# Splitting a place in a list at 64 instead of 128: smaller one-hots, more values, results written in two halves

## The chip, the cores and the metric

The kernel runs on one core of a Trainium2 chip. A core has a matrix engine (TensorE, in the profile PE, with its weight loads shown apart as PEld), a vector engine (VectorE, DVE), a scalar engine (ScalarE, ACT), a general engine (GpSimd, POOL) and SyncE (SP), which issues most of the transfers. Each engine works through its own list of instructions in order and waits on semaphores for the others. The metric is the device time of one execution in microseconds (us), the median of several runs. The profile comes from one further execution.

## What is computed

Four graph-attention layers over 4096 nodes with 256 features and one adjacency matrix of 4096 x 4096, in which about one entry in 256 is set, more of them for nodes with low numbers. Each layer normalises, projects, forms a softmax over the neighbours of every node, and adds the result to x. The first layer stands for all:

```python
h = jnp.maximum(_layernorm(x, axis=-1), 0.0)
h = h @ W.T + b_W
e = (h @ a1)[:, None] + (h @ a2)[None, :] + b_a[0]
e = jnp.where(e > 0, e, 0.2 * e)
scores = jnp.where(adj > 0, e, NEG_INF)
x = x + jax.nn.softmax(scores, axis=1) @ h
```

The second layer ends with an elu, the third has four heads of 64 features, the fourth subtracts a second softmax of the negated scores and projects both.

## The kernel before

Targets are taken in tiles of 128 nodes (32 tiles), four tiles to a block. A target tile is worked on in one of two ways. Densely: all 32 source tiles are multiplied, with a mask. By lists: only those sources that some node of the target tile has as a neighbour. Target tiles with low numbers have many neighbours and stay dense (four blocks in the first layer); for the 28 tiles of blocks 1 to 7 the first layer also makes a list of sources, and the later layers use it. The first four source tiles are always taken whole; 28 source tiles (JT) remain to be listed.

For a list, the number of a used source has to stand at its place: source k-th in the list goes to partition k mod 128 and column k div 128 of a tile idx of 128 partitions and CAPS[T] columns (6 to 12). Each column of idx then drives one indirect transfer on POOL: 128 rows of the feature table (L1228) or of the mask table (L928) are gathered with it.

The function `list_sources` does this for one block of four target tiles. It is a Python generator: a pump advances it by one `yield` at a time in between the steps of the dense and listed multiplications, so that its instructions are issued among theirs. `seen` tells which sources are used; two small matmuls and some additions give every source its place in the list (posi); an unused source gets a place beyond any list. Then

- L857 and L858 split posi into its low part (and with 127) and its high part (shift by 7), and L860 and L862 turn both into f16;
- L865 makes val, a one-hot of the high part over MAXCAP = 12 columns, and L869 multiplies it with the source's own number (code);
- L875, in `one_hot`, makes first, a one-hot of the low part over 128 places, for half of the 28 source tiles at a time: two such instructions for each target tile, 56 in all, made one ahead of their use, in two buffers;
- L900 multiplies them: for each target tile, 28 matmuls of 128 sources each, first as the stationary and val as the moving operand, are added up in PSUM, so that the number of each source lands on its place. 28 tiles with 28 matmuls make 784;
- L910 writes the sum, with an offset and as integers, to idx.

The constants place (0 to 127, repeated) and lists (0 to 11, repeated), against which L865 and L875 compare, are written by POOL at the start in `list_constants` (L790, L794). POOL's order is the program's own; the instructions of the other engines are ordered by a scheduler when the kernel is compiled, so a change in one part can move others by some places.

Around the lists run the other parts of the first layer: L1303 loads pieces of the adjacency matrix, L1322 makes the mask of them (DVE), L1032 weighs mask and scores (DVE, tile s_p), L1068 multiplies weights and features (PE, tile s_acc), L716 and L748 transpose and project nodes for the next layer, L1119 to L1122 end a target tile. L580 is a group of 16 small matmuls for the third layer's weights, L640 of four for a bias, L829 and L830 the two matmuls that count list places. L1093 is the multiplication of the third layer.

Of the kernel before, what the change touches and what calls it, by code (L numbers as in the profile page):

```python
# [8 lines left out]
F32 = mybir.dt.float32  # L9
F16 = mybir.dt.float16  # L10
# [3 lines left out]
ALU = mybir.AluOpType  # L14
# [3 lines left out]
P = 128  # L18
# [5 lines left out]
IT = IB // P  # L24
# [432 lines left out]
JT = NT - DP  # L457
# [6 lines left out]
MAXCAP = max(CAPS[TS0:])  # L464
OFFS = [sum(CAPS[TS0:T]) for T in range(NT + 1)]
NLIST = OFFS[NT]
HALF = N // 2
# [12 lines left out]
def list_layers(ctx: ExitStack, tc: tile.TileContext, a: dict, out: bass.AP, flag):  # L480

    nc = tc.nc
# [8 lines left out]
    ps_mm = ctx.enter_context(tc.tile_pool(name="s_mm", bufs=2, space=PSUM))  # L491
# [15 lines left out]
        tri, onesb, pattern=[[1, P]], compare_op=ALU.is_gt, fill=0.0, base=0, channel_multiplier=-1  # L507
# [278 lines left out]

    def list_constants(pool):

        place = pool.tile([P, P, JT // 2], F16, name="place")
        nc.gpsimd.iota(  # L790
            place, pattern=[[1, P], [0, JT // 2]], base=0, channel_multiplier=0, allow_small_or_imprecise_dtypes=True
        )
        lists = pool.tile([P, MAXCAP, JT * IT], F16, name="lists")
        nc.gpsimd.iota(  # L794
            lists,
            pattern=[[1, MAXCAP], [0, JT * IT]],
            base=0,
            channel_multiplier=0,
            allow_small_or_imprecise_dtypes=True,
        )  # L800

        code = pool.tile([P, JT * IT], F16, name="code")
        n = (NT // 2 - DP) * IT
        for part, tiles, base in ((code[:, 0:n], NT // 2 - DP, DP * P - HALF), (code[:, n:], NT // 2, 1)):
            nc.gpsimd.iota(
                part,
                pattern=[[CH * P, tiles // CH], [1, CH], [0, IT]],
                base=base,
                channel_multiplier=CH,
                allow_small_or_imprecise_dtypes=True,  # L810
            )
        sums = []
        for k in range(2):
            t = pool.tile([P, NT // 2 + JT, IT], F32, name=f"sums_{k}")
            nc.gpsimd.memset(t[:, 0 : NT // 2, :], 0.0)
            sums.append(t)
        return place, lists, code, sums

    def list_sources(ib, seen, pool, consts):

        n = JT * IT
        place, lists, code, sums = consts
        half = JT // 2
        used = pool.tile([P, JT, IT], F16, name=f"used_{ib}", tag="used")
        nc.vector.tensor_scalar(used, seen, 0.0, None, op0=ALU.is_gt)
        yield 4.0
        uf = used.rearrange("p j t -> p (j t)")
        pre = ps_mm.tile([P, 2, JT, IT], F32, name=f"pre_{ib}", tag="mm")
        nc.tensor.matmul(pre[:, 0].rearrange("p j t -> p (j t)"), lhsT=tri, rhs=uf, start=True, stop=True)  # L829
        nc.tensor.matmul(  # L830
            pre[:, 1].rearrange("p j t -> p (j t)"), lhsT=onesb, rhs=uf, start=True, stop=True
        )
        yield

        z = NT // 2
        nc.vector.tensor_copy(sums[0][:, z:, :], pre[:, 1])
        pos = pool.tile([P, JT, IT], F32, name=f"pos_{ib}", tag="pos")
        nc.vector.tensor_sub(pos, pre[:, 0], sums[0][:, z:, :])
        k, a = 1, 0
        while k < JT:  # L840
            nc.vector.tensor_add(
                sums[1 - a][:, z:, :], sums[a][:, z:, :], sums[a][:, z - k : z + JT - k, :]
            )
            k, a = 2 * k, 1 - a
        yield
        t0 = ib * IT - TS0
        nc.vector.tensor_sub(
            over[:, t0 : t0 + IT], sums[a][:, z + JT - 1, :], places[:, t0 : t0 + IT]
        )
        nc.vector.tensor_add(pos, pos, sums[a][:, z:, :])  # L850

        nc.vector.tensor_scalar(pos, pos, 8192.0, None, op0=ALU.add)
        posi = pool.tile([P, JT, IT], I32, name=f"posi_{ib}", tag="posi")
        nc.vector.scalar_tensor_tensor(posi, used, -8192.0, pos, op0=ALU.mult, op1=ALU.add)
        yield
        low = pool.tile([P, 2, JT, IT], I32, name=f"low_{ib}", tag="low")
        nc.vector.tensor_scalar(low[:, 0], posi, P - 1, None, op0=ALU.bitwise_and)  # L857
        nc.vector.tensor_scalar(low[:, 1], posi, 7, None, op0=ALU.logical_shift_right)  # L858
        lof = pool.tile([P, IT, JT], F16, name=f"lof_{ib}", tag="lof")
        nc.vector.tensor_copy(lof, low[:, 0].rearrange("p j t -> p t j"))  # L860
        hib = pool.tile([P, n], F16, name=f"hib_{ib}", tag="hib")
        nc.vector.tensor_copy(hib, low[:, 1].rearrange("p j t -> p (j t)"))  # L862
        yield
        val = pool.tile([P, MAXCAP, n], F16, name=f"val_{ib}", tag="val")
        nc.vector.tensor_tensor(  # L865
            val, lists, hib.unsqueeze(1).to_broadcast([P, MAXCAP, n]), op=ALU.is_equal
        )
        yield
        nc.vector.tensor_tensor(val, val, code.unsqueeze(1).to_broadcast([P, MAXCAP, n]), op=ALU.mult)  # L869
        yield 4.0  # L870

        def one_hot(T, j):

            first = pool.tile([P, P, half], F16, name=f"first_{T}_{j}", tag="first", bufs=2)
            nc.vector.tensor_tensor(  # L875
                first,
                place,
                lof[:, T % IT, j : j + half].unsqueeze(1).to_broadcast([P, P, half]),
                op=ALU.is_equal,
            )  # L880
            return first


        ahead = [(ib * IT + t, j) for t in range(IT) for j in (0, half)]
        firsts = [one_hot(*ahead[0])]
        yield 4.0
        for t in range(IT):
            T = ib * IT + t
            cap = CAPS[T]
            ps = None  # L890
            for j in range(JT):
                if j % half == 0:
                    first = firsts.pop()
                    ahead.pop(0)
                    if ahead:
                        firsts.append(one_hot(*ahead[0]))
                    yield
                if ps is None:
                    ps = ps_mm.tile([P, MAXCAP], F32, name=f"idx_ps_{T}", tag="mm")
                nc.tensor.matmul(  # L900
                    ps[:, 0:cap],
                    lhsT=first[:, :, j % half],
                    rhs=val[:, 0:cap, j * IT + t],
                    start=(j == 0),
                    stop=(j == JT - 1),
                )
                if j % 7 == 6:
                    yield
            idx = keep.tile([P, cap], I32, name=f"idx_{T}", tag=f"idx_{T}")
            nc.vector.tensor_scalar(idx, ps[:, 0:cap], float(HALF), None, op0=ALU.add)  # L910
            index[T] = idx
            yield

# [331 lines left out]
    with ExitStack() as phase:  # L1245
# [33 lines left out]
        half = CH // 2  # L1279
# [31 lines left out]
        def mask_chunk(ib, c):  # L1311

            load()
            if ib == 0:
                behind(c)
            m = (
                mpre[:, :, ib * IB : (ib + 1) * IB]
                if c == 0
                else mpool.tile([P, CH, IB], U8, name=f"s_m_{ib}_{c}", tag="m")
            )  # L1320
            for h, raw in enumerate(loaded[ib, c]):
                nc.vector.tensor_scalar(m[:, h * half : (h + 1) * half, :], raw, 0.0, None, op0=ALU.is_gt)  # L1322
            if c > 0 or ib in MASKS_IN:
                nc.sync.dma_start(mask_rows(ib, c * CH), m)
            if ib > 0:
                if c == 0:
                    seen[ib] = lists_p.tile([P, JT, IT], F32, name=f"seen_{ib}", tag="seen", bufs=4)
                else:
                    nc.vector.tensor_reduce(
                        seen[ib][:, (c - 1) * CH : c * CH, :].rearrange("p j t -> p (j t)"),  # L1330
                        m.rearrange("p j i -> p (j i)")
                        .bitcast(I32)
                        .rearrange("p (t w) -> p t w", w=P // 4),
                        AX.X,
                        ALU.max,
                    )
                if c == NCH - 1:
                    push(lists_q, list_sources(ib, seen[ib], lists_p, consts))
            return m
# [31 lines left out]
        for b in range(1, 4):  # L1371
            load_x(b)
        consts = list_constants(lists_p)
        for _ in L0.making:
            pass
# [4 lines left out]
        for ib in range(DENSE[0]):  # L1380
            for step in block(ib).plan():
                plan.append(step)
                if ib * NT + step[1] >= LISTED0:
                    n = 1 + step[1] % 2
# [25 lines left out]
    for l in (1, 2, 3):  # L1410
# [37 lines left out]
        if l == 3:  # L1448
            one = Unit(L, 0, IT, NT, all_sources(L, 0, IT, [0], 1), big="growb", heads=[0])
            two = Unit(L, 0, IT, NT, all_sources(L, 0, IT, [1], 1), big="growb", heads=[1], like=one)  # L1450
            first = one.plan() + two.plan()
        else:
            per = L.H
            first = []
# [88 lines left out]
```

## Time and profile before

| | |
|---|---|
| Median of 3 runs | 1701.94 us (1697.17 to 1703.21) |
| The profiled execution itself | 1796.08 us |
| its span, first to last instruction | 1794.3 us |
| granted TensorE clock, mean over the span | 0.97 |
| List matmuls L900 | 784, first at 114.5, last at 499.1 us |
| Indirect transfers that read idx | 715 for features, 105 for masks |
| Adjacency loads L1303 | 128 of 512 KB |

The profiled execution is longer than the runs; durations of single instructions are taken from it and sums are made against it. A page of a profile gives, for each group of instructions, the line, the engine, the operation, the tiles written and read, shapes, count, the busy time in us and the mean of one in ns, and after the bar the time for which the engine stood idle just before, with what ended that. The chain of waits follows the work that ended last back to what released it. A share of busy time is an average over stages that have different limits, so it is the stage of the lists, from about 90 to 510 us, that has to be read. Matmul ends are modelled, so a burst of matmuls is best measured from its first start to the start of what follows.

### The profile page before, as it was taken

What the parts mean: (1) busy time and instruction counts of PE and PEld (TensorE: products, weight loads), DVE (VectorE), ACT (ScalarE), POOL (GpSimd) and SP (SyncE); (2) the same over time, 40 slices, a digit from 0 to 9 for tenths busy, and PEclk for the clock granted to TensorE, in tenths of its full rate; (3) what the DMA queues carried; (4) which work ended last, traced back from release to release, by engine and by line L of the source; (5) the groups of instructions that cost most, each with busy time, mean ns of one, the idle gap of its engine ahead of it and who ended that gap; (6) DMA issues with size and microseconds to landing.
All of it is one profiled execution on the core that took longest, in us unless ns stands there. A gap on an engine that the chain in (4) does not pass through costs nothing.

```text
span 1794.3 us, 29158 instructions
## 1 busy us (share of the span) xinstructions
PE 1660.2 (93%) x9268; PEld 1384.3 (77%) x9268; DVE 1319.1 (74%) x3908; ACT 631.0 (35%) x1915; POOL 960.5 (54%) x930
## 2 busy tenths in 40 slices
PE   6998899799889999888999999988889999999997
PEld 4886777678778778676577878788888888888876
DVE  6787899777744676556788888877785566777755
ACT  5630010020120232333467666788884011111101
POOL 8836666646535656553353444444561666655453
PEclk9999999999879999989999999999999999999999
DMA  7888778853244444543233332323342665666553
GB/s 258 301 299 281 242 244 251 264 143 110 60 135 138 134 117 134 147 132 106 82 94 86 90 90 81 98 82 83 99 116 75 197 208 175 183 180 178 160 165 107
DMA packets 152237, 274.70 MB, mean 153 GB/s; under 512 B 21423, under 2 KB 75340, under 8 KB 152076
## 3 DMA queue, kind: packets, MB, share of 16 engines
q0 software_dynamic: 45584, 130.39, 26.8%
q1 hardware_dynamic: 105656, 141.83, 24.2%
q8 instruction: 77, 1.26, 0.3%
q14 instruction: 84, 0.69, 0.1%
q10 hardware_dynamic: 836, 0.53, 0.1%
HBM read 231.76 MB, written 40.90 MB: 152 GB/s over the span
## 4 chain that ended last, share of the span: by engine, by line
PE 78%; DVE 8%; issue 4%; DMA 3%; POOL 3%; ACT 2%; another core or an unknown queue 2%; SPq 0%; POOLq 0%; DVEq 0%; ACTq 0%
PE s_acc L1068 44%; PE s_accm L1093 20%; PE s_pj L748 8%; DVE s_p L1032 3%; PE idx_ps L900 2%; PE s_tp L716 2%; PE s_sT L966 2%; DMA s_gg<-table,idx 1%; DMA s_raw<-in_adjT 1%; ACT s_p L1018 1%; DVE s_m L1322 1%; POOL s_z L702 1%; POOL s_gg L1228 1%; DVE s_p L1041 0%
## 5 line engine op out<-in xcount | busy, mean ns | idle before, releaser
L1228 POOL DMA_INDIRECT s_gg<-table,idx x715 | 757.9, 1060 | 733.5 <-PE s_acc L1068 228.6
L1032 DVE SCALAR_TENSOR_TENSOR s_p<-s_grow,s_gg,mlist 128x128 f32<-128x128 f32 x994 | 310.1, 346 | 143.0 <-PE s_acc L1068 85.9
L1068 PE MATMUL s_acc<-s_gg,s_p 128*128 128x257 f32 x1430 | 353.8, 390 | 9.9 <-DVE s_p L1032 7.8
L1068 PEld LDWEIGHTS s_acc<-s_gg,s_p 128*128 128x128 f32 x1430 | 270.5, 194 | 53.6 <-DVE s_p L1032 12.6
L1068 PE MATMUL s_acc<-g,s_p 128*128 128x257 f32 x1152 | 292.5, 397 | 14.2 <-DVE s_p L1032 5.3
L1068 PEld LDWEIGHTS s_acc<-g,s_p 128*128 128x128 f32 x1152 | 220.0, 198 | 49.7 <-issue 12.3
L1032 DVE SCALAR_TENSOR_TENSOR s_p<-s_grow,pre,mpre 128x128 f32<-128x128 f32 (+1 forms) x576 | 189.2, 369 | 49.4 <-PE s_acc L1068 30.5
L1093 PE MATMUL s_accm<-s_p,s_gg 128*65 128x128 f32 x1744 | 204.7, 273 | 1.7 <-issue 1.6
L1068 PE MATMUL s_acc<-s_gs,s_p 128*128 128x257 f32 x896 | 203.6, 380 | 0.0
L1032 DVE SCALAR_TENSOR_TENSOR s_p<-s_grow,s_gs,s_ms 128x512 f32<-128x512 f32 x224 | 161.9, 748 | 50.7 <-PE s_accm L1093 24.7
L748 PE MATMUL s_pj<-s_w,s_hT 128*128 128x259 f32 (+3 forms) x640 | 175.9, 417 | 24.9 <-ACT s_hT L718 9.5
L1093 PEld LDWEIGHTS s_accm<-s_p,s_gg 128*65 128x65 f32 x1744 | 193.2, 138 | 5.3 <-issue 2.8
L1018 ACT ACTIVATE s_p<-s_grow,s_minus,s_gg 128x128 f32<-128x128 f32 x436 | 186.7, 485 | 25.9 <-PE s_accm L1093 15.0
L1068 PE MATMUL s_acc<-pre,s_p 128*128 128x257 f32 x768 | 184.0, 384 | 5.5 <-ACT s_y L1179 3.5
L1068 PEld LDWEIGHTS s_acc<-s_gs,s_p 128*128 128x128 f32 x896 | 169.4, 190 | 24.7 <-issue 0.6
L972 ACT ACTIVATE s_grow<-s_sT 128x256 f32<-128x256 f32 (+2 forms) x136 | 46.8, 367 | 379.3 <-PE s_sT L966 260.9
L748 PEld LDWEIGHTS s_pj<-s_w,s_hT 128*128 128x128 f32 x640 | 126.3, 205 | 56.4 <-ACT s_hT L718 14.2
L1068 PEld LDWEIGHTS s_acc<-pre,s_p 128*128 128x128 f32 x768 | 144.5, 192 | 28.4 <-ACT s_y L1179 3.9
L928 POOL DMA_INDIRECT mlist<-mask_t,idx x105 | 122.1, 1162 | 65.1 <-issue 30.0
L1093 PE MATMUL s_accm<-s_p,pre 128*65 128x128 f32 (+1 forms) x928 | 122.2, 286 | 2.6 <-issue 2.5
L1093 PEld LDWEIGHTS s_accm<-s_p,pre 128*65 128x65 f32 x928 | 105.1, 139 | 21.0 <-issue 18.3
L1018 ACT ACTIVATE s_p<-s_grow,s_minus,pre 128x128 f32<-128x128 f32 x224 | 95.0, 485 | 23.2 <-issue 18.9
(126 smaller groups left out, 1743.5 us busy)
## 6 DMA issues: line engine op xcount, KB each, us to landing
s_raw<-in_adjT SPq DMA_DIRECT2D x128, 512.0 KB
s_gs<-table SPq DMA_DIRECT2D x28, 516.0 KB
s_gg<-table,idx POOLq DMA_INDIRECT x715
mask_t<-s_m SPq DMA_DIRECT2D x35, 256.0 KB
table<-s_g SPq DMA_DIRECT2D x28, 258.0 KB
s_ms<-mask_t SPq DMA_DIRECT2D x28, 256.0 KB
table<-s_m SPq DMA_DIRECT2D x21, 256.0 KB
table<-g SPq DMA_DIRECT2D x8, 516.0 KB
```

Source lines behind the costliest of these rows:

```text
L702: (nc.gpsimd if L.l == 0 else nc.vector).tensor_scalar(z, x[:, T, :], mv[:, k, 0:1], 0.0, op0=ALU.subtract, op1=ALU.max)
L716: nc.tensor.transpose(tp[:, c, :], zs[k][:, c * P : (c + 1) * P], ident)
L748: nc.tensor.matmul(ps, lhsT=hT[:, c, :], rhs=L.w[:, c, k * (D + 6) : k * (D + 6) + cols], start=(c == 0), stop=(c == 1),)
L900: nc.tensor.matmul(ps[:, 0:cap], lhsT=first[:, :, j % half], rhs=val[:, 0:cap, j * IT + t], start=(j == 0), stop=(j == JT - 1),)
L928: nc.gpsimd.indirect_dma_start(out=mlist[:, OFFS[T] + k, :], out_offset=None, in_=mask_t[T // IT], in_offset=bass.IndirectOffsetOnAxis(ap= ...
L966: nc.tensor.transpose(ps[:, h - h0, it, :], L.s[:, T0 + it, h : h + 1].to_broadcast([P, P]), ident)
L972: nc.scalar.activation(grow[:, h1:h2, :], ps[:, h1 - h0 : h2 - h0].rearrange("p h a b -> p h (a b)"), AF.Exp, scale=scale,)
L1018: nc.scalar.activation(w[:, h, :], u.grow[:, h, :], AF.Relu, scale=g[h][:, n - 1 : n], bias=minus)
L1032: nc.vector.scalar_tensor_tensor(p[:, k, :], u.grow[:, h, :], g[k][:, n - 1 : n], m, op0=ALU.min if L.l == 3 and h == 1 else ALU.max, op1= ...
L1068: nc.tensor.matmul(u.accs[it][h], lhsT=p[:, k, it * P : (it + 1) * P], rhs=g[k][:, 0:n], start=first, stop=last,)
L1093: nc.tensor.matmul(u.regions[h], lhsT=g[k][:, 0 : DH + 1], rhs=p[:, k, :],  start=first and (u.nt > 1 or h == 0), stop=last, skip_group_ch ...
L1228: nc.gpsimd.indirect_dma_start(out=wide, out_offset=None, in_=L.table, in_offset=bass.IndirectOffsetOnAxis(ap=index[T][:, k : k + 1], axis=0),
```

## The change

The place is split at 64: the low six bits choose one of 64 places, the rest one of 2 x MAXCAP = 24 columns. The one-hots first have half their size, the values val twice theirs; a matmul has 64 stationary columns and twice the moving columns (12 to 24), and its result has 64 partitions. Even columns of it belong to partitions 0 to 63 of idx, odd ones to 64 to 127, so the result is written with two instructions, one for each half. What idx holds is the same.

```diff
-        place = pool.tile([P, P, JT // 2], F16, name="place")
+        place = pool.tile([P, P // 2, JT // 2], F16, name="place")
...
-        lists = pool.tile([P, MAXCAP, JT * IT], F16, name="lists")
+        lists = pool.tile([P, 2 * MAXCAP, JT * IT], F16, name="lists")
...
-        nc.vector.tensor_scalar(low[:, 0], posi, P - 1, None, op0=ALU.bitwise_and)
-        nc.vector.tensor_scalar(low[:, 1], posi, 7, None, op0=ALU.logical_shift_right)
+        nc.vector.tensor_scalar(low[:, 0], posi, P // 2 - 1, None, op0=ALU.bitwise_and)
+        nc.vector.tensor_scalar(low[:, 1], posi, 6, None, op0=ALU.logical_shift_right)
...
-        val = pool.tile([P, MAXCAP, n], F16, name=f"val_{ib}", tag="val")
+        val = pool.tile([P, 2 * MAXCAP, n], F16, name=f"val_{ib}", tag="val")
         nc.vector.tensor_tensor(
-            val, lists, hib.unsqueeze(1).to_broadcast([P, MAXCAP, n]), op=ALU.is_equal
+            val, lists, hib.unsqueeze(1).to_broadcast([P, 2 * MAXCAP, n]), op=ALU.is_equal
         )
         yield
-        nc.vector.tensor_tensor(val, val, code.unsqueeze(1).to_broadcast([P, MAXCAP, n]), op=ALU.mult)
+        nc.vector.tensor_tensor(val, val, code.unsqueeze(1).to_broadcast([P, 2 * MAXCAP, n]), op=ALU.mult)
...
-            first = pool.tile([P, P, half], F16, name=f"first_{T}_{j}", tag="first", bufs=2)
+            first = pool.tile([P, P // 2, half], F16, name=f"first_{T}_{j}", tag="first", bufs=2)
...
-                    ps = ps_mm.tile([P, MAXCAP], F32, name=f"idx_ps_{T}", tag="mm")
+                    ps = ps_mm.tile([P // 2, 2 * MAXCAP], F32, name=f"idx_ps_{T}", tag="mm")
                 nc.tensor.matmul(
-                    ps[:, 0:cap],
+                    ps[:, 0 : 2 * cap],
                     lhsT=first[:, :, j % half],
-                    rhs=val[:, 0:cap, j * IT + t],
+                    rhs=val[:, 0 : 2 * cap, j * IT + t],
...
-            nc.vector.tensor_scalar(idx, ps[:, 0:cap], float(HALF), None, op0=ALU.add)
+            for k in range(2):
+                nc.vector.tensor_scalar(
+                    idx[k * P // 2 : (k + 1) * P // 2, :], ps[:, k : 2 * cap : 2], float(HALF), None, op0=ALU.add
+                )
```

The two iotas on POOL and the broadcasts of the comparisons follow these sizes.

More of the change, by code (lines that the diff above doesn't have):

```diff
@@ L787, in list_constants @@
     def list_constants(pool):
-        place = pool.tile([P, P, JT // 2], F16, name="place")
+        place = pool.tile([P, P // 2, JT // 2], F16, name="place")
         nc.gpsimd.iota(
-            place, pattern=[[1, P], [0, JT // 2]], base=0, channel_multiplier=0, allow_small_or_imprecise_dtypes=True
+            place, pattern=[[1, P // 2], [0, JT // 2]], base=0, channel_multiplier=0, allow_small_or_imprecise_dtypes=True
         )
-        lists = pool.tile([P, MAXCAP, JT * IT], F16, name="lists")
+        lists = pool.tile([P, 2 * MAXCAP, JT * IT], F16, name="lists")
         nc.gpsimd.iota(
             lists,
-            pattern=[[1, MAXCAP], [0, JT * IT]],
+            pattern=[[1, 2 * MAXCAP], [0, JT * IT]],
             base=0,
@@ L877, in one_hot @@
                 place,
-                lof[:, T % IT, j : j + half].unsqueeze(1).to_broadcast([P, P, half]),
+                lof[:, T % IT, j : j + half].unsqueeze(1).to_broadcast([P, P // 2, half]),
                 op=ALU.is_equal,
```

## The prediction

> **What bounds the kernel now.** I read the whole page first, then the busy time by stretches, then only the stretch in which the changed code runs. The lists are made between 90 and 500 us; past 510 us no instruction that the change touches is left. In the page, section 1 gives the engines and the groups give the places; in the table by stretches, the columns are the stretch, its length, and the busy time of PE, PE's weight loads, DVE, ACT and POOL with counts, then TensorE's clock, the DMA share and GB/s.
>
> ```profile
> PE 1660.2 (93%) x9268; PEld 1384.3 (77%) x9268; DVE 1319.1 (74%) x3908; ACT 631.0 (35%) x1915; POOL 960.5 (54%) x930
> ```
>
> ```profile
> 100.00:150.00 50.00, 46.94 (x281) 39.78 (x280) 45.77 (x98) 11.43 (x43) 21.24 (x17) 1.00 0.89 297
> 150.00:200.00 50.00, 42.04 (x258) 34.97 (x257) 40.16 (x88) 1.43 (x6) 35.77 (x30) 1.00 0.84 264
> 200.00:250.00 50.00, 44.67 (x251) 36.85 (x251) 42.56 (x116) 7.44 (x26) 31.45 (x26) 0.90 0.72 227
> 250.00:300.00 50.00, 46.92 (x313) 39.94 (x313) 46.21 (x111) 7.12 (x26) 32.15 (x26) 1.00 0.86 251
> ```
>
> PE is busy for 84 to 94% of these stretches and DVE for 80 to 92%: two in-order engines that feed each other, both nearly full. The groups of the stretch 100 to 510 us show what the lists cost in it:
>
> ```profile
> L875 DVE TENSOR_TENSOR first<-place,lof 128x1792 f16<-128x1792 f16 x56 | 60.8, 1085 | 7.1 <-PE idx_ps L900 4.1 <-PE s_acc L1068 2.9
> L900 PEld LDWEIGHTS <-first 128*128 128x128 f16 x784 | 58.7, 158 | 13.1 <-DVE val L869 2.3 <-issue 2.1 <-DVE first L875 2.0
> L900 PE MATMUL idx_ps<-val,first 128*128 128x6 f16 (+6 forms) x784 | 55.7, 202 | 3.7 <-DVE val L869 1.9 <-DVE first L875 1.6 <-ACT s_hT L718 0.2
> L865 DVE TENSOR_TENSOR val<-lists,hib 128x1344 f16<-128x1344 f16 x7 | 5.9, 849 | 0.0
> L869 DVE TENSOR_TENSOR val<-val,code 128x1344 f16<-128x1344 f16 x7 | 5.9, 848 | 0.0
> L910 DVE TENSOR_SCALAR idx<-idx_ps 128x6 int32<-128x6 f32 (+6 forms) x28 | 4.5, 162 | 38.1 <-remote 16.4 <-PE idx_ps L900 12.0 <-PE s_tp L716 6.7
> ```
>
> The last column is the engine's idle time before the group. DVE's eviction of an index tile (L910) waits 38.1 us, mostly for PE; the dense weighing (L1032) waits for PE too. The reverse, PE waiting for DVE, sums to about 20 us in the table of waits. So PE is the tighter of the two. The chain of waits over 90 to 500 us agrees: PE's s_acc 40.4%, PE's idx_ps 8.2%, DVE's s_p 5.1%, DVE's first only 2.0%. Of 410 us that is 33.6 us of idx_ps (0.60 of its 55.7 us busy) and 8.2 us of first (0.135 of its 60.8). I use these two shares as the worth of a microsecond saved or added on PE's list matmuls and on DVE's list work.
>
> How close the list matmuls stand is read from the timeline (start, length, operation), in two cuts:
>
> ```profile
> 289.60 0.95 PE L900 MATMUL idx_ps<-val,first 128*128 128x6 f16 x14
> 290.41 0.68 PE L1068 MATMUL s_acc<-s_gg,s_p 128*128 128x257 f32 x2
> ...
> 543.71 5.37 PE L1068 MATMUL s_acc<-s_gs,s_p 128*128 128x257 f32 x24
> 549.00 1.94 PE L580 MATMUL s_wa<-s_av,s_wt 64*128 64x2 f32 x16
> 550.88 5.47 PE L1068 MATMUL s_acc<-s_gs,s_p 128*128 128x257 f32 x24
> ```
>
> Fourteen list matmuls take 290.41 - 289.60 = 0.81 us, 58 ns each. Their moving side is 6 to 12 columns, so it is the load of 128 strided weight columns that sets this pace.
>
> [...]f16 loads are fast: the contiguous one (L829) takes 97 ns, the strided one of L900 158, an fp32 one of 128 columns 192 (L1068). [...]the trace has 192 ns for 128 and 138 for 65 fp32 columns (L1093), 0.86 ns a column[...].
>
> **The change part by part.**
>
> One-hots (L875), removed half: a 16-bit tensor_tensor of 1792 elements takes 1083 ns, of 1344 (L865) 850: 0.52 ns an element. 896 elements: 1083 - 466 = 617 ns. 56 x 0.466 = -26.1 us of DVE.
>
> Values (L865, L869): 2688 instead of 1344 elements, +699 ns each; 14 x 0.699 = +9.8 us of DVE.
>
> Results (L910): 28 more evictions at 0.16 us = +4.5. The second writes partitions 64 to 127[...]. In the timeline small DVE operations of 0.16 us follow at 0.08, so a lost overlap costs 0.08: 28 x 2 x 0.08 = +4.5. Lowest: 28 x 0.08 = +2.2, no hold; highest +9.0, which I take. DVE in all: -26.1 + 9.8 + 9.0 = -7.3 us (bounds -7 and -14). At 0.135 this is -1.0 us (to -1.9). If DVE alone set the pace it would be -7 to -14.
>
> Weight loads (L900): 784 loads of 64 columns. [...]64 x 0.86 = 55 ns by the fp32 slope[...], against 58 now. 784 x -0.003 = -2.4 us. Lower bound: if f16 columns load at half that price the next limit is the spacing of tiny matmuls. Four one-column ones (L640) take 0.24 us with 164 ns each, so (0.24 - 0.164)/3 = 25 ns; with 30 ns, 784 x -0.028 = -22 us. Upper: stride costs the 128-column load 158 - 97 = 61 ns; half of it on top of 55 makes 86 ns, 784 x 0.028 = +22 us. I take 55[...].
>
> Moving side: 12 to 24 columns instead of 6 to 12, hidden beneath the load; nothing.
>
> [...]in the compiled order the list matmuls stand in 74 runs between dense ones (71 before). [...]24 dense matmuls at 0.217 us (76 in 16.48 in the chain) from 543.71 would end at 548.92, the next starts at 549.00: 0.08 us. And the first load, which now starts 0.22 us ahead of its matmul (118.68 against 118.90 in the timeline), lies bare: 138 ns for 65 columns, of which some 0.09 us stays, since matmuls start before a load's record ends. The exit of L580, 1.88/16 = 0.118 us a matmul to the end, shows no loss. 74 x 0.17 = +12.6 us. Bounds: 0.06 without bare load (+4.4), 0.27 with 0.10 at the exit (+20).
>
> PE in all: +12.6 - 2.4 = +10.2 us; at 0.60 on the path, +6.1.
>
> Constants: POOL writes place with half the elements and lists with twice. lists took 1.85 us for 1344, 1.38 ns an element: place -1.24, lists +1.85, so POOL's first s_z, which is on the chain at 10.02 us, starts +0.6 us later. Bounds -0.5 (place's 4.62 us all per element) and +1.9 (place no shorter). Later POOL work keeps its order.
>
> Places in the order: the scheduler moves PE instructions by up to 42 and DVE's by up to 43 places within the list section, none after. I count it at nothing, give or take 3 us. Memory is neutral: place and the two first buffers give back 5376 bytes a partition, lists and val take 5376.
>
> Sum: +6.1 - 1.0 + 0.6 = +5.7 us against the profiled execution of 1796.08 us (span 1794.3), 0.32%. The median of the runs, 1701.94, is 0.948 of that execution; the same share gives 1707 us. About 0.5%, 8.5 us, is what a measurement of this kernel can tell from no change.
>
> **The rivals.**
>
> Cheap loads (0.25): [...]PE -22 + 4.4 to 12.6, at 0.60 -5.6 to -10.6, with DVE -1 and POOL +0.6: -6 to -11 us; where the loads are wholly on the path, to -17. About 1692. For it: a strided load's fastest record, 137 ns, is only 56 above the 81 of one column. Against: fp32 loads at 0.86 a column. It decides from a spacing of about 40 ns downward.
>
> DVE's relief counts in full (0.12): first comes sooner, PE's 20 us of waits for DVE shrink by half. -10 and +6: 1698. Against: the 38.1 us for which L910 waits for PE would only grow.
>
> Dear loads or switches (0.21): the strided 64-column load at 86 ns, +22 + 12.6 = +35 us of PE, at 0.60 +21: 1722. It decides once spacing passes 65 ns or a run's switch 0.3 us.
>
> **How the numbers follow.** The forecast, spacing kept and switches paid, has 0.42, own range 1701 to 1714. It gives 0.01 faster, 0.27 same, 0.14 slower; cheap loads 0.22 faster, 0.03 same; DVE's relief 0.06 and 0.06; dear ones 0.21 slower. Faster 0.29, same 0.36, slower 0.35. The range runs from the middle of the cheap case, 1690, to the upper part of the dear one, 1727.
>
> **What would show it.** first at about 617 ns, val at 1549, 56 evictions; the load of 64 columns at 130 to 140 ns and 14 matmuls in about 0.8 us; a gap of 0.15 to 0.2 us before each run of list matmuls, with the first load no longer ahead. PE busy per list stretch up, L910's wait for PE longer. I am wrong if the spacing falls to 30 ns, if no gap is seen at the entries, or if DVE's waits for PE shrink instead.

## The result, and the profile after

The changed kernel takes 1787.78 us (median of 4 runs, 1785.86 to 1788.19) against 1699.56 us for the kernel before on the same chip: a ratio of 1.0518, interval 1.0488 to 1.0549. It is 88 us slower, far outside the predicted range. Runs that lay over 1.5% above the fastest of their kernel, three in all, are left out of the medians and ratios below.

Chips differ here: the kernel before takes some 1700 us on some, 1783 on a second and 1794 on a third, and its first profile (span 1794.3 us) is of the longer sort, so a further profile of it, `control`, with a span of 1701.1 us, is set beside that of the changed kernel (1786.1 us), and every ratio below is against the kernel before on the experiment's own chip.

In the page, the engines' totals; first the changed kernel, then control:

```profile
PE 1715.1 (96%) x9268; PEld 1436.2 (80%) x9268; DVE 1311.7 (73%) x3936; ACT 632.4 (35%) x1915; POOL 943.5 (53%) x930
```

```profile
PE 1626.1 (96%) x9268; PEld 1369.9 (81%) x9268; DVE 1323.4 (78%) x3908; ACT 633.6 (37%) x1915; POOL 959.9 (56%) x930
```

The number of matmuls is the same, and PE is busy for 89 us longer, about as much as the kernel is slower. DVE did get 12 us of work less. Next, the busy time by stretches (columns as in the prediction: PE, weight loads, DVE, ACT, POOL, then TensorE's granted clock, DMA share, GB/s), the changed kernel first:

```profile
100.00:200.00 100.00, 97.08 (x481) 80.24 (x480) 78.38 (x181) 12.37 (x46) 50.81 (x43) 0.93 0.85 272
200.00:300.00 100.00, 96.50 (x484) 79.67 (x484) 72.53 (x208) 14.33 (x52) 44.50 (x42) 0.91 0.66 199
300.00:400.00 100.00, 93.12 (x455) 76.52 (x454) 75.21 (x187) 8.48 (x30) 56.76 (x51) 0.91 0.74 219
400.00:500.00 100.00, 98.53 (x470) 80.43 (x469) 57.58 (x154) 9.34 (x37) 42.06 (x41) 0.85 0.37 100
```

```profile
100.00:200.00 100.00, 94.22 (x573) 79.16 (x572) 89.63 (x191) 11.31 (x41) 61.64 (x51) 0.98 0.93 299
200.00:300.00 100.00, 95.01 (x594) 80.28 (x593) 92.44 (x235) 14.73 (x53) 62.93 (x52) 0.97 0.83 249
300.00:400.00 100.00, 94.70 (x577) 79.94 (x576) 87.21 (x226) 14.61 (x53) 64.10 (x55) 1.00 0.73 208
400.00:500.00 100.00, 93.25 (x519) 77.88 (x518) 71.55 (x219) 21.43 (x78) 56.70 (x56) 0.93 0.47 120
```

PE is as full as before, but gets through fewer matmuls: 481 instead of 573 in the first of these stretches. DVE falls from 90 to 78% busy in the first and from 92 to 73% in the second: it waits. And the clock, 0.93 to 1.00 before, is 0.85 to 0.93: a second loss beside the longer instructions. The groups from 100 to 560 us (busy us, mean ns of one, idle time before) show the changed code; the changed kernel, then control:

```profile
L900 PE MATMUL idx_ps<-val,first 128*64 128x12 f16 (+6 forms) x784 | 104.1, 268 | 1.9 <-DVE val L869 1.5 <-ACT s_hT L718 0.4
L900 PEld LDWEIGHTS <-first 128*64 128x64 f16 x784 | 97.3, 211 | 30.0 <-issue 21.6 <-DVE val L869 2.2 <-DVE s_p L1035 1.7
...
L875 DVE TENSOR_TENSOR first<-place,lof 128x896 f16<-128x896 f16 x56 | 34.8, 621 | 22.5 <-PE idx_ps L900 22.1
...
L865 DVE TENSOR_TENSOR val<-lists,hib 128x2688 f16<-128x2688 f16 x7 | 10.9, 1556 | 0.0
L869 DVE TENSOR_TENSOR val<-val,code 128x2688 f16<-128x2688 f16 x7 | 10.9, 1551 | 0.0
...
L911 DVE TENSOR_SCALAR idx<-idx_ps 64x6 int32<-64x6 f32 (+6 forms) x56 | 8.8, 158 | 72.2 <-PE idx_ps L900 71.7
```

```profile
L875 DVE TENSOR_TENSOR first<-place,lof 128x1792 f16<-128x1792 f16 x56 | 60.6, 1082 | 2.9 <-PE idx_ps L900 2.9
...
L900 PEld LDWEIGHTS <-first 128*128 128x128 f16 x784 | 58.3, 157 | 9.9 <-DVE val L869 2.3 <-issue 1.0
L900 PE MATMUL idx_ps<-val,first 128*128 128x6 f16 (+6 forms) x784 | 55.3, 201 | 2.3 <-DVE val L869 1.9 <-ACT s_hT L718 0.4
...
L910 DVE TENSOR_SCALAR idx<-idx_ps 128x6 int32<-128x6 f32 (+6 forms) x28 | 4.4, 157 | 15.6 <-PE idx_ps L900 15.6
```

A load of half as many columns takes 211 ns instead of 157, and the list matmuls keep PE busy for 104.1 instead of 55.3 us. DVE now waits 71.7 + 22.1 us for them, where it waited 15.6 + 2.9. How they stand one after the other is seen in the timeline of PE (start, length):

```profile
198.82 1.80 PE L900 MATMUL idx_ps<-val,first 128*64 128x14 f16 x14
200.55 2.00 PE L1071 MATMUL s_acc<-g,s_p 128*128 128x257 f32 x8
202.48 0.99 PE L900 MATMUL idx_ps<-val,first 128*64 128x14 f16 x7
...
206.50 3.66 PE L1071 MATMUL s_acc<-g,s_p 128*128 128x257 f32 x8
210.09 0.99 PE L900 MATMUL idx_ps<-val,first 128*64 128x14 f16 x7
```

Fourteen list matmuls take 200.55 - 198.82 = 1.73 us, 124 ns each with the exit, where they took 58. And eight dense matmuls that take 202.48 - 200.55 = 1.93 us take 210.09 - 206.50 = 3.59 us a moment later: 449 ns each. The row by stretches shows the granted clock there, 0.50, and before it:

```profile
196.00:206.50 10.50, 10.50 (x65) 8.77 (x66) 5.36 (x13) 0.00 (x0) 7.79 (x8) 1.00 0.67 216
206.80:210.10 3.30, 3.30 (x9) 2.10 (x8) 2.56 (x5) 0.00 (x0) 1.97 (x3) 0.50 0.94 289
```

The list matmuls don't slow down with it: their spacing is 117 ns inside such spells as outside. What the spells cost is paid by the other matmuls.

From the start times of PE's matmuls between 100 us and the last list matmul, the difference adds up. In the table, times in ns are medians. The entry is from the last dense start to the first list start, the first spacing from there to the second list matmul, the spacing that within a run of list matmuls, the exit from the last list start to the next dense one. "Half" counts those of some 1010 spacings between dense matmuls that are about 433 instead of 217 ns.

| | entry ns | first spacing ns | spacing ns | exit ns | runs of list matmuls | half | last list matmul, us |
|---|---|---|---|---|---|---|---|
| control | 217 | 29 | 60 | 61 | 71 | 15 | 461.8 |
| changed | 310 | 138 | 117 | 195 | 74 | 113 | 549.3 |

The two list stretches as rows, control first:

```profile
100.00:461.80 361.80, 345.28 (x2131) 292.69 (x2130) 320.74 (x803) 52.06 (x190) 232.72 (x198) 0.99 0.76 227
100.00:549.30 449.30, 434.22 (x2137) 357.73 (x2135) 313.93 (x837) 52.70 (x195) 219.83 (x198) 0.90 0.61 183
```

The list stretch ends 549.3 - 461.8 = 87.5 us later, which is the whole difference of the spans (85.0). The list matmuls with their exits take 98.8 us instead of 45.9, and the entries 74 x 0.093 = 6.9 us more. Of the 52.9 us, 43.6 are the spacing within the runs (mean 118.9 instead of 57.2 ns), and 74 x 0.109 = 8.1 of these are the first spacings; the exits hold another load's excess, 74 x 0.057 = 4.2 us, and some 5 us beyond it. The 98 more half-clock spacings are 98 x 0.216 = 21 us. So about 40 us are slower weight loads, 20 the entries, first spacings and exits, 21 the clock. PE's idle time is no longer than before, 449.30 - 434.22 = 15.1 us against 361.80 - 345.28 = 16.5; the 6 or 7 us that are left lie in entries longer than the median and in other matmuls that are slowed. This divides one pair of executions; which of these terms hangs on what is for the experiments.

### The profile page after: what moved, and what is told of

It is laid out like the page before. It is cut to its first block, busy times and chain, and to the rows that moved or that the text cites. A ratio compares the mean times of both kernels' runs of the same rounds, so it can differ in the third digit from the quotient of the medians.

```text
span 1786.1 us, 29194 instructions
## 1 busy us (share of the span) xinstructions
PE 1715.1 (96%) x9268; PEld 1436.2 (80%) x9268; DVE 1311.7 (73%) x3936; ACT 632.4 (35%) x1915; POOL 943.5 (53%) x930
## 4 chain that ended last, share of the span: by engine, by line
PE 48%; DVE 2%; ACT 1%; DMA 1%; issue 0%; ACTq 0%; DVEq 0%
PE s_acc L1071 23%; PE s_accm L1096 20%; PE s_pj L748 3%; PE s_sT L969 1%; DMA s_gg<-table,idx 1%; ACT s_p L1021 1%; DVE s_p L1035 1%; PE s_tp L716 0%; PE s_oT L1158 0%; DVE s_p L1044 0%; DVE s_y L1187 0%; DVE s_out L1138 0%; ACT mlist L1243 0%; ACT s_g L783 0%; DVE s_y L1165 0%
## 5 line engine op out<-in xcount | busy, mean ns | idle before, releaser
L1231 POOL DMA_INDIRECT s_gg<-table,idx x715 | 743.6, 1040 | 737.5 <-PE s_acc L1071 292.1
L1035 DVE SCALAR_TENSOR_TENSOR s_p<-s_grow,s_gg,mlist 128x128 f32<-128x128 f32 x994 | 316.1, 348 | 110.5 <-PE s_acc L1071 61.4
L1071 PE MATMUL s_acc<-s_gg,s_p 128*128 128x257 f32 x1430 | 350.2, 388 | 5.3 <-DVE s_p L1035 5.3
L1071 PE MATMUL s_acc<-g,s_p 128*128 128x257 f32 x1152 | 311.7, 417 | 10.8 <-DVE s_p L1035 6.6
L1071 PEld LDWEIGHTS s_acc<-g,s_p 128*128 128x128 f32 x1152 | 230.1, 206 | 49.7 <-DVE s_p L1035 9.7
L748 PE MATMUL s_pj<-s_w,s_hT 128*128 128x259 f32 (+3 forms) x640 | 168.5, 406 | 6.3 <-ACT s_g L783 3.5
L931 POOL DMA_INDIRECT mlist<-mask_t,idx x105 | 117.8, 1122 | 72.4 <-issue 28.6
L900 PEld LDWEIGHTS <-first 128*64 128x64 f16 x784 | 97.3, 211 | 30.0 <-issue 21.6
```

What stands on the lines that cost most here:

```text
L748: nc.tensor.matmul(ps, lhsT=hT[:, c, :], rhs=L.w[:, c, k * (D + 6) : k * (D + 6) + cols], start=(c == 0), stop=(c == 1),)
L900: nc.tensor.matmul(ps[:, 0 : 2 * cap], lhsT=first[:, :, j % half], rhs=val[:, 0 : 2 * cap, j * IT + t], start=(j == 0), stop=(j == JT - 1),)
L931: nc.gpsimd.indirect_dma_start(out=mlist[:, OFFS[T] + k, :], out_offset=None, in_=mask_t[T // IT], in_offset=bass.IndirectOffsetOnAxis(ap= ...
L1035: nc.vector.scalar_tensor_tensor(p[:, k, :], u.grow[:, h, :], g[k][:, n - 1 : n], m, op0=ALU.min if L.l == 3 and h == 1 else ALU.max, op1= ...
L1071: nc.tensor.matmul(u.accs[it][h], lhsT=p[:, k, it * P : (it + 1) * P], rhs=g[k][:, 0:n], start=first, stop=last,)
L1231: nc.gpsimd.indirect_dma_start(out=wide, out_offset=None, in_=L.table, in_offset=bass.IndirectOffsetOnAxis(ap=index[T][:, k : k + 1], axis=0),
```

## The experiments

The theory after the result, A in what follows: an f16 load of 64 columns costs more a column than one of 128, most of all when the columns are strided. The rivals: the 64-column matmuls set the pace themselves or by the switches between them and the 128-column matmuls around them (B); DVE's side has turned slower; the clock alone.

**control** is the kernel before, unchanged, for a profile on a chip of the kind that the timed runs had.

> The kernel before once more, profiled on the chip of the following runs, because its only profiled execution took 1796 us where its timed runs took 1700. If the profile lengthens this kernel by itself, it is 1790 to 1800 us again, and the changed kernel's profile (1788, equal to its runs) can't be set against it stretch by stretch. If that one execution was an odd one, this one is about 1700 us and shows where the 95 us of the first profile lay; the lists should then end near 490 us or earlier.

It took 1702.87 us, with the numbers shown above. In the lists nothing stood differently from the first profile (spacing 60, entry 217, exit 61 ns, 71 runs; L875 1082 ns against 1085). That profile's extra 93 us were not in longer instructions of these kinds. The list stretch held 37 of them (its last list matmul is at 499.1 instead of 461.8 us): PE's idle time in it was 39.6 us against 16.5, and its half-clock spacings 33 against 15. Where the rest lay stays open.

**cols65** makes the stationary side 65 columns wide. The load has one column more than in the changed kernel and the same stride, so what goes with 64 columns alone shows as a difference from it.

```diff
-        place = pool.tile([P, P // 2, JT // 2], F16, name="place")
+        place = pool.tile([P, P // 2 + 1, JT // 2], F16, name="place")
...
-            first = pool.tile([P, P // 2, half], F16, name=f"first_{T}_{j}", tag="first", bufs=2)
+            first = pool.tile([P, P // 2 + 1, half], F16, name=f"first_{T}_{j}", tag="first", bufs=2)
...
-                    ps = ps_mm.tile([P // 2, 2 * MAXCAP], F32, name=f"idx_ps_{T}", tag="mm")
+                    ps = ps_mm.tile([P // 2 + 1, 2 * MAXCAP], F32, name=f"idx_ps_{T}", tag="mm")
```

> The changed kernel with 65 stationary columns in place of 64 (the 65th place is never hit)[...]. Theory A (the ordinary strided load costs about 116 ns a matmul[...]): spacing stays at 110 to 120 ns, the time at 1770 to 1790. Theory B[...]: spacing falls to about 60 ns, the time to about 1700.

Measured: 1748.87 us, ratio 1.0266 (1.0232 to 1.0301). The list of what touches `first` in it (duration of one: lowest, median, highest; first and last start):

```profile
L900 PEld LDWEIGHTS <-first x784: 192/214/223, 114.0 to 524.7; 128*65 128x65 f16 x196
```

The load is as long with 65 columns (median 214 ns, 212 in the changed kernel), and the spacing is 118 ns. So it isn't what sets 64 columns apart from 65 that makes the load slow. Entry is 217, the first spacing 29 and the exit 119 ns: with 65 columns the entry costs nothing, the first spacing is short as in control, and the exit is one ordinary spacing. That leaves for the switch to 64 columns and back 310 - 217 = 93 ns at each entry, 138 - 29 = 109 at each first spacing and 195 - 119 = 76 at each exit: 0.28 us a run, and 74 x 0.278 = 20.6 us in all. The two profiled executions stand 1786.1 - 1766.0 = 20.1 us apart.

The medians stand 39 us apart, more than was expected (1770 to 1790 us for this kernel): the slow load without these switches accounts for 48 of the 88 us, its own half-clock spells included. The profiled execution was the longest of the four, with 83 half-clock spacings and a mean granted clock of 0.965; the others have 0.973 to 0.978, the changed kernel 0.957 to 0.963. The switches' 20.6 us are half of the other 40; the rest goes with the clock, but how much of that loss the switches bring about isn't shown.

**contig64** keeps 64 columns, and lays the columns of each one-hot side by side.

```diff
-            first = pool.tile([P, P // 2, half], F16, name=f"first_{T}_{j}", tag="first", bufs=2)
+            first = pool.tile([P, half, P // 2], F16, name=f"first_{T}_{j}", tag="first", bufs=2)
...
-                lof[:, T % IT, j : j + half].unsqueeze(1).to_broadcast([P, P // 2, half]),
+                lof[:, T % IT, j : j + half].unsqueeze(2).to_broadcast([P, half, P // 2]),
...
-                    lhsT=first[:, :, j % half],
+                    lhsT=first[:, j % half, :],
```

> The changed kernel with the one-hots stored source tile by source tile, so that the 64 stationary columns lie side by side (DVE then compares against an operand that repeats along the inner dimension, about 1.08 us in place of 0.62). Theory A, in its form that the stride is what makes the ordinary load dear: the spacing falls to 53 to 65 ns, the time to 1710 to 1740. Theory B: the spacing stays near 116 ns and the time is 1785 or more.

Measured: 1711.83 us, ratio 1.006 (1.0038 to 1.0082).

```profile
L900 PEld LDWEIGHTS <-first x784: 106/114/156, 112.5 to 468.4; 128*64 128x64 f16 x196
...
L875 DVE TENSOR_TENSOR first<-place,lof x56: 1054/1084/1139, 103.4 to 466.4; 128x896 f16<-128x896 f16 x56
```

The load falls from 212 to 114 ns, the spacing from 117 to 33 (53 to 65 were expected), and nearly all of the loss is gone, though the switches stay (entry 310, first spacing 53, exit 117 ns with a spacing of 33) and though DVE pays for it: lof repeated along the innermost axis costs 1084 ns for 896 elements instead of 621, 56 x 0.46 = 26 us. So the load of 64 columns is dear through its stride (a spacing of 117 ns strided, 33 adjacent); having 64 columns doesn't make it dear alone. The half-clock spacings fall from 113 to 32 as well.

**cols128** keeps the split at 64, but loads the one-hots within tiles of 128 columns, whose upper half is set to zero once. PE's side is then that of the kernel before, and DVE has its lighter work.

```diff
+        wide = []
+        for k in range(2):
+            t = pool.tile([P, P, JT // 2], F16, name=f"wide_{k}")
+            nc.gpsimd.memset(t[:, P // 2 :, :], 0.0)
+            wide.append(t)
...
-            first = pool.tile([P, P // 2, half], F16, name=f"first_{T}_{j}", tag="first", bufs=2)
+            first = wide[j // half]
             nc.vector.tensor_tensor(
-                first,
+                first[:, 0 : P // 2, :],
```

To make room, lists is half as long and compared twice, and two integer tiles are reused in place.

> The changed kernel with the one-hots laid into 128 stationary columns, the upper 64 zero (to find room for them, lists has half its length and is compared twice, and two small integer tiles are written in place): [...]with the halved DVE one-hots kept. Theories A and B both give a spacing of 58 to 60 ns and the time of the kernel before or a little less, 1685 to 1702. If the loss lies elsewhere (values, split eviction, constants), it stays above 1740.

Measured: 1708.24 us (19 runs), ratio 1.0031 (1.0019 to 1.0044).

```profile
L909 PEld LDWEIGHTS <-wide x784: 137/159/179, 111.1 to 467.4; 128*128 128x128 f16 x196
...
L884 DVE TENSOR_TENSOR wide<-place,lof x56: 606/622/678, 99.7 to 463.9; 128x896 f16<-128x896 f16 x56
```

With 128 columns the load is the old one, 159 ns at a spacing of 60, though DVE makes the same small one-hots: the slow load is PE's matter alone. And the prediction's DVE saving, present here without its price, buys nothing: DVE's busy time is 8.6 us less than in control (1314.8 against 1323.4), but the kernel is 0.3% slower, where the same or a little less was expected. PE stood idle in its list stretch for 22.7 us (16.5 in control), 5.2 of them for val (1.9), which takes twice as long at the head of each block.

**pairs128** and **pairs64** ask which version is best. Both lay the columns side by side, and lof is written twice over, as pairs, so that no operand of the comparison repeats single elements along its innermost axis. The first keeps the split at 128, the second has it at 64.

```diff
-        lof = pool.tile([P, IT, JT], F16, name=f"lof_{ib}", tag="lof")
+        lof = pool.tile([P, IT, JT, 2], F16, name=f"lof_{ib}", tag="lof")
...
-            first = pool.tile([P, P, half], F16, name=f"first_{T}_{j}", tag="first", bufs=2)
+            first = pool.tile([P, half, P], F16, name=f"first_{T}_{j}", tag="first", bufs=2)
...
-                lof[:, T % IT, j : j + half].unsqueeze(1).to_broadcast([P, P, half]),
+                lof[:, T % IT, j : j + half].unsqueeze(2).to_broadcast([P, half, P // 2, 2]),
```

> The kernel before (split at 128) with the one-hots stored source tile by source tile, so that the 128 stationary columns lie side by side; the low parts are written twice, as pairs, so that DVE's comparison keeps its 16-bit rate. Theory stride (the strided load sets 58 ns): the spacing falls to 25 to 35 ns, PE loses 18 to 26 us of list work, the time is 1675 to 1692. If the comparison falls back[...] it takes about 2 us, DVE gains 50 us and the time is above 1725. If PE's list work is not what the stretch waits for, the time stays within 1695 to 1705.

> The changed kernel (split at 64) in the same layout: contiguous columns, comparison of 0.62 us. [...]Theory stride: against the run with contiguous columns and the slow comparison (1711.8 us) DVE is relieved of 26 us, so 1690 to 1705; the split at 64 should then still be level with or slower than the split at 128 in this layout by 5 to 15 us, for the entries and exits (0.15 us in 71 runs is 11 us).

Both were run again on another chip, beside the changed kernel:

> Split at 128 with contiguous columns. On the other chip PE's list work fell by 24 us (spacing 27 ns) and PE stood idle 15 us longer, and the time stayed. If the stretch is bound by PE here, 1675 to 1690 on a chip where the kernel before takes 1700; if DVE's work takes over as the limit, 1692 to 1702.

> Split at 64 with contiguous columns and the comparison at the 16-bit rate. On the other chip it was 26 us slower than the same layout split at 128. [...]it is 10 to 25 us above the split at 128 here too.

| | first chip: us, ratio | second chip: us, ratio |
|---|---|---|
| before | 1794.15 | 1782.81 |
| pairs128 | 1792.22, 0.9976 (0.9949 to 1.0002) | 1770.19, 0.9947 (0.9917 to 0.9976) |
| pairs64 | 1818.38, 1.016 (1.0084 to 1.0236) | 1789.50, 1.0031 (1.0000 to 1.0063) |

Of `first` in pairs128 and then in pairs64, on the first chip:

```profile
L900 PEld LDWEIGHTS <-first x784: 95/96/153, 114.2 to 492.1; 128*128 128x128 f16 x196
...
L875 DVE TENSOR_TENSOR first<-place,lof x56: 1067/1082/1134, 105.6 to 489.0; 128x1792 f16<-128x1792 f16 x56
```

```profile
L900 PEld LDWEIGHTS <-first x784: 106/114/157, 111.7 to 516.0; 128*64 128x64 f16 x196
...
L875 DVE TENSOR_TENSOR first<-place,lof x56: 601/618/662, 102.5 to 510.8; 128x896 f16<-128x896 f16 x56
```

DVE's comparison costs what it did in the kernel before (1082 ns), and the load of 128 columns falls from 159 to 96 ns, the spacing from 60 to 26. So PE has some 20 us of list work less than in the kernel before, and little of it comes out: pairs128 is the fastest kernel of the study, by 0.5% on one chip and by an amount that its interval doesn't separate from none on the other, and of the cases expected the first chip has the one in which the time stays. PE stands idle there for 54.6 us of the list stretch (39.6 in the first profile of the kernel before). With the stride gone on both sides, the split at 64 still loses 26.2 and 19.3 us to that at 128. About 14 us of this are switches (93 ns at the entry and 120 - 26 = 94 at the exit, 74 times), 5 to 9 the spacing (33 against 26 ns by the medians, 39.9 against 27.5 by the means, first spacings included), and 4 and 7 the half-clock spacings (63 against 45, 54 against 20).

**fill4** asks whether the half clock hangs on how few columns the list matmuls stream. Each takes the values of all four target tiles, four times the moving columns, and of the result only the wanted tile's columns are used; idx is the same.

```diff
-                    rhs=val[:, 0 : 2 * cap, j * IT + t],
+                    rhs=val[:, 0 : 2 * cap, j * IT : (j + 1) * IT],
```

> The changed kernel with four times as many moving columns (all four target tiles of the block are multiplied, only the own one is used), 48 to 96 in place of 12 to 24; the load still sets the spacing of about 117 ns. Theory clock ([...]113 of 1017 spacings of s_acc): fewer than 50 halved spacings, time 1765 to 1778. If moving columns do not count, it stays at 1785 to 1792.

> The changed kernel with four times the moving columns, beside the changed kernel itself. Theory clock: about 50 halved spacings of s_acc against about 110, and 10 to 25 us less than the changed kernel. If the clock spells are only a companion of the longer stretch: the same time within 5 us.

> The changed kernel once more, as the reference for the three that follow on the same chip: 1.045 to 1.055 of the kernel before, with 110 or so halved spacings of s_acc in the list stretch.

On the first chip fill4 took 1831.59 us, ratio 1.0238 (1.0159 to 1.0318), without the changed kernel beside it. On the second, the changed kernel again (after_again) took 1845.40 us, 1.0351 (1.0279 to 1.0424), less of a loss than the 1.045 that was expected at least: 63 us where the first measurement had 88. The same fill4 there (fill4_b) took 1822.08, 1.0196 (1.0125 to 1.0267): 23 us less for more columns. Busy time from 100 to 550 us there, after_again and then fill4_b:

```profile
100.00:550.00 450.00, 428.10 (x2087) 350.55 (x2086) 309.82 (x823) 49.91 (x183) 217.14 (x195) 0.90 0.59 180
```

```profile
100.00:550.00 450.00, 427.18 (x2158) 354.20 (x2157) 320.71 (x857) 54.14 (x198) 229.01 (x204) 0.93 0.59 182
```

The mean clock in this stretch is 0.93 instead of 0.90 and 71 more matmuls get through at the same busy time. The spacing within a run stays 117 ns with 48 to 96 moving columns as with 12 to 24 (it is 33 in contig64, with 12 to 24), so the strided load still sets it; the half-clock spacings fall from 94 to 58, which is 36 x 0.216 = 7.8 us of the 15.1 by which the list stretch ends earlier (542.2 instead of 557.3 us). PE's idle time in it is no shorter (22.8 and 21.9 us), and the list matmuls stand in 78 runs instead of 74. By the profiles' records of the granted clock, 60 us of this stretch are at half clock instead of 94 (control: 10). What comes before the spells differs too. All three of control follow more than 1 us of idle PE within 7 us; of the 17 in after_again, 12 follow at least 14 list matmuls with no more than 0.33 us of idle PE, and of the 11 in fill4_b 7 do. The two profiled executions stand 12.3 us apart, less than the medians. So how much the list matmuls stream does bear on the clock; the exact rule stays open, and so does the part of the 23 us that the two profiles don't hold. The switches aren't needed for it: cols65 has 83 half-clock spacings without them, contig64 32 with them.

**runs14** lets a target tile's list matmuls run in 56 longer runs instead of 74, for fewer switches.

```diff
-                if j % 7 == 6:
+                if j % 14 == 13:
```

> The changed kernel with the list matmuls issued 14 at a time instead of 7, so that 56 runs of them stand between dense matmuls in place of 74. Theory switch (0.23 us for entry and exit together beyond what the kernel before pays): 18 fewer runs save 4 us, 1782 to 1786. If a switch costs more than the spacing shows[...], 1770 to 1780; if runs of 14 hold up the dense work, 1790 or more.

It took 1864.54 us, ratio 1.0388 (1.0305 to 1.0472) on a chip on which the changed kernel was not run; its ratio was 1.0351 and 1.0518 on two others. No gain is seen, though 18 switches x 0.28 = 5 us could be one; its 106 half-clock spacings show no help for the clock either (113 and 94 in the two profiles of the changed kernel). With the chips differing as they do, it decides nothing.

## Why the prediction was wrong

- **The step that failed is the price of the weight loads.** The prediction put 55 ns on a list matmul, by the slope of fp32 loads (192 ns for 128 columns, 138 for 65), and called 86 ns the upper bound, by adding half of what stride cost the 128-column load. It is 117 ns, 57 more than in control where 3 fewer were forecast. In cols65, where the switches have no part, the spacings within the runs sum to 77.9 us against 40.8 and the exits to 8.8 against 4.3: some 41 us instead of -2.4. This step alone takes the forecast out of its range: at the prediction's own rate, (41 + 12.6) x 0.60 = 32 us, about 1732.
- **The slope didn't give the price of these loads.** 64 columns stand 33 ns apart when adjacent and 117 at a step of 28 bytes, and 55 is neither. The slope came from two groups of fp32 loads, L1068 and L1093, but the same trace has fp32 loads of 128 columns with a median of 141 ns (L716) and 137 (L966), so these durations don't give a price by columns. And the bound took stride to cost the same a column at 64 columns as at 128. By the load records it costs (212 - 114) / 64 = 1.5 ns a column at 64 and (159 - 96) / 128 = 0.49 at 128; by the spacing (117 - 33) / 64 = 1.3 and (60 - 26) / 128 = 0.27, the latter perhaps too low, for 26 ns is next to the 25 of the tiny matmuls of L640, and something other than the load may set it. The trace of before has f16 loads of 128 columns only (L900, L829, L830), so it could not show this.
- **That a column would cost more at 64 than at 128 was right**, though for f16 it was the author's estimate, which the trace of before did not show: strided, 128 columns load in 159 ns, 64 in 212 and, in cols65, 65 in 214; adjacent, 128 in 96 and 64 in 114. Where between 65 and 128 columns this turns was not shown.
- **The switches were forecast in kind, and cost the upper bound.** 0.17 us a run was forecast, 0.27 the bound; 0.28 is measured against cols65, 74 x 0.278 = 20.6 us instead of 12.6. The 0.17 us was the author's estimate from L580 and a bare first load; what PE does at a switch was not shown. The places were not quite right: the entry holds only 93 ns of the 170, the second list matmul comes late too, 138 ns after the first instead of 29, and the exit, where L580 showed no loss, costs 76 ns (against cols65) to 84 (contig64, 117 - 33).
- **The worth of PE's time was too low.** The prediction multiplied PE's excess by 0.60, the share of the list matmuls' busy time that lay on the chain. That is a share, not a rate of exchange. With PE busy for 93 to 98% of the stretch, the whole of what PE gained, 89 us of busy time by the engines' totals, came out in a span 85 us longer. Two of the readings behind it were loose: of the 38.1 us that L910 waited, 21.8 were for PE and 16.4 "remote" (another core or an unknown queue), and control has 15.6, all for PE; and PE's waits for DVE in that stretch sum to 16.9 us, not 20.
- **The clock was missing.** No step named it. About 21 us are dense matmuls at half clock that ran at full before, 433 ns apart instead of 217. That a PE which is busy by the profile can still lose the clock is what the changed kernel shows (0.50 from 206.8 to 210.1 us, after 10.5 us in which PE was busy throughout), and that it loses less of it with more columns streamed is what fill4_b shows.
- **DVE's terms were right and worth nothing.** One-hots 621 ns (617 forecast), values 1556 and 1551 (1549), 56 evictions of 158. Two evictions, which write from partition 0 and from partition 64, take 0.33 us together, two full lengths, so the second starts after the first has ended; most instructions behind the second start some 190 ns after it, where those behind L910 in control start after some 80. Not even the -1.0 us put on all of it came: cols128, with DVE's saving and none of PE's price, is 0.3% slower. That also speaks against the rival in which DVE's relief counts in full.
- **The other small terms** don't show in the time. The constants had the wrong sign: place falls from 4.62 to 2.38 us and lists grows only from 1.81 to 2.51, so POOL's first s_z starts at 8.71 instead of 9.96 us, 1.25 earlier where 0.6 later was forecast. The first list matmul still starts 1.3 us later, but between executions of the changed kernel alone it moves from 111.9 to 114.2 us. That the wider moving side is hidden agrees with cols128: 12 to 24 columns at a spacing of 60 ns, as with 6 to 12 in control. The places in the order are not separable.

Of the rivals, the one of dear loads had the right direction and decided from 65 ns upward, but its 1722 us was built on the same bound of 86 ns and the same rate of 0.60. The cheap case, 30 ns, is what contig64 has, in a layout that the change doesn't use.

## What to carry to other kernels

The price of a weight load here hung on the number of its columns and their stride together: take it from a trace that shows both, and where none does, let the bound be wide, since stride alone was worth a factor of 2.3 in the spacing at 128 f16 columns (60 ns against 26) and 3.5 at 64 (117 against 33). Before a stationary operand is made smaller than 128 columns, ask whether its load set the pace; if so, lay its columns side by side first, which gained 0.5% on one of two chips where halving lost. And here a small saving on DVE, which waits, was worth nothing, while each microsecond added on PE, which was full, cost a microsecond. The reverse doesn't follow: in pairs128, 20 us taken from PE came out as 2 and 13 us, with PE waiting more.

## What the runs showed of the hardware that was not expected

- Spacing of matmuls with few moving columns, f16: 128 strided columns 60 ns, 128 adjacent 26, 64 strided 117, 65 strided 118, 64 adjacent 33. The stride was 28 bytes (14 elements). At half clock, 117 stays 117.
- Each run of 64-column matmuls between 128-column neighbours costs 0.28 us with strided columns (entry 93, first spacing 109, exit 76 ns, against 65 columns) and 0.21 with adjacent ones (93, 24 and 94, against 128 columns); a run of 65-column ones has the entry and first spacing of 128 columns, 217 and 29 ns.
- Bursts of matmuls that stream 12 to 24 columns go with spells of half clock in the dense matmuls around them (113 of about 1010 spacings, 15 before), though PE is 93 to 98% busy by the profile; four times the columns at the same pace left 58 where there had been 94, on another chip. In the changed kernel 12 of 16 such spells begin with no more than 0.33 us of idle PE in the 7 us before.
- A 16-bit comparison of 896 elements took 621 ns with an operand broadcast along an outer axis, 1084 with it repeated element by element along the innermost, and 618 with it written as pairs: the pair is enough to keep the pace.
- A DVE instruction that writes from partition 64 after one that wrote from partition 0 starts 172 ns after it (it lasts 158), and the next instruction some 190 ns after that; without such a change the follower starts after some 80.
- Chips differ: the median of the kernel before was 1699.56 and 1700.87 us in two sets of runs, and 1782.81 and 1794.15 on two other chips. Single instructions have the same length (L875 1082 and 1085 ns in the two profiles); the mean granted clock was 0.980 to 0.986 in the runs near 1700 us and 0.966 to 0.978 in those at 1783.
